# Reordering the last batch of a cross-attention kernel: sums ahead of value columns, small operations and a mask moved up

## The chip, the core and the metric

The kernel runs on one core of a Trainium2 chip. The metric is the device time of one launch in microseconds (us); three runs of the kernel before gave 453.07, 457.52 and 457.72, so its median is 457.52 us. All data are 32-bit floats. The engines have queues of their own[...]: TensorE (PE; loads of its stationary operand are shown apart as PEld), VectorE (DVE), ScalarE (ACT), GpSimd (POOL) and SyncE (SP), which here issues the DMA transfers.

## What is computed

For each of 8 batches: `S` = 112 queries with 320 channels attend to 371 text tokens and to 4 prompt tokens of a context of 375 tokens with 512 channels, in 20 heads of 16 channels.

```python
text_ehs, ip_ehs = encoder_hidden_states[:, :-4], encoder_hidden_states[:, -4:]
q, k_t, v_t = heads(hidden_states @ W_q), heads(text_ehs @ W_k), heads(text_ehs @ W_v)
probs_t = softmax(einsum('bhsd,bhtd->bhst', q, k_t) * attn_scale)
text_out = einsum('bhst,bhtd->bhsd', probs_t, v_t)
k_ip, v_ip = heads(ip_ehs @ W_k_ip), heads(ip_ehs @ W_v_ip)
attn_scores = einsum('bhsd,bhnd->bhsn', q, k_ip) * attn_scale
qsem = l2norm(einsum('bhst,bte->bhse', probs_t, text_ehs))
sem = einsum('bhse,bne->bhsn', qsem, l2norm(ip_ehs))
probs_ip = softmax(attn_scores + 0.5 * sem) * spatial_mask
ip_out = einsum('bhsn,bhnd->bhsd', probs_ip, v_ip)
out = (text_out + ip_out) @ W_out + b_out + hidden_states
```

The second softmax, over the four prompt tokens, needs the length of `qsem` for each query and head, and so a sum over all text tokens that is known only when a head's products are done.

## The kernel before

**Groups and products.** A batch's 20 heads are done in five groups (`g` = 0 to 4) of four heads each. `scores` (L573) multiplies queries by keys into one PSUM bank a head; `probabilities` (L591) takes the maximum (L595, VectorE), the exponent (L599, ScalarE) into the tile `p`, of which there are three buffers (L597), and sends it to the tile `xg` by a DMA a head (L602). When all four have landed, `transposed` (L606) makes one VectorE transpose of 128 by 1536 (L610). `multiplied` (L616) then does 12 blocks of four products (L629) on TensorE, each head into a bank of its own: columns 0 to 370 of a bank belong to the quadratic form behind the length of `qsem`, and the last 21, the "value columns", hold four prompt sums, the softmax's denominator `z` and the 16 text output channels. Its moving operand `u` holds the values of one group at a time; `placed` (L547) copies those of the next group over them on POOL, a third at a time, as soon as TensorE has done the blocks that read that third.

**After a group's products.** `value_sums` (L639) copies the value columns of each bank to `pvs` on ScalarE (L642). `reduced` (L673) multiplies columns 0 to 370 by `p` and sums them into `ss`, one custom VectorE instruction a head (L677). In the last batch some heads go another way, `shared` (L644): ScalarE copies value columns and bank out (L661, L662), POOL multiplies (L666), ScalarE sums (L670). VectorE and ScalarE never read one bank at the same time: whichever comes first in the program is waited for by the other.

**The end of a batch.** `finish` (L690) is a generator; each `next` or `run` issues one piece. Its pieces for a whole batch in the last batch's manner (`bd` given) are: (1) `xb`, the residual plus bias, on POOL, and `z2`, `rn` on VectorE; (2) a square root on ScalarE (L724), which needs a table load, and a load of the exponent's table after it; (3) six small VectorE operations from `zr` to `fu` (L741 to L748); (4) an exponent (L752); (5) three small VectorE operations up to the weights `w` (L756 to L760), and the division `divided` on POOL (L731); (6) a TensorE transpose of `w` and ScalarE's copy of it, `wT` (L768, L772); (7) products with the block diagonal `bd` into `ps_a` and ScalarE's copy `aT` (L778, L781, L789); (8) the output projection `ps_o` (L796); (9) `ob`, the sum with `xb`; (10) the transfer out. `ob` has one buffer. `own_channels` (L532) masks `bd`, the prompt values of batches 6 and 7, to block diagonals on POOL, by a memset and two selects.

**The last batch.** Batches 0 to 6 run in a loop with all engines in program order but POOL. For batch 7 POOL joins them (L1020), so every queue there holds the order of the program text, loop L1039 to L1090 and what follows it. That batch computes in group `g` the scores of group `g + 2` (`places`, L1045: after which block which heads), ends batch 6 in pieces (`run(before, ...)`) between its own, and does its own end in two parts: `first`, heads 0 to 15, begun after group 3, and `last`, heads 16 to 19, after group 4. `awake` (L366) is three multiplies whose result nobody uses.

Of the kernel before, what the change touches and what calls it, by code (L numbers as in the profile page):

```python
# [8 lines left out]
F32 = mybir.dt.float32  # L9
AF = mybir.ActivationFunctionType  # L10
ALU = mybir.AluOpType
# [9 lines left out]
def kernel(  # L21
# [503 lines left out]
        )  # L525

    def load_prompt_values_by_head():
        bd = io.tile([P, NT, E], F32, tag="ct", name="bd")[:HN, :2, :CP]
        nc.sync.dma_start(bd[:, :, :C], vipx.rearrange("b h n c -> (h n) b c"))
        return bd  # L530

# [74 lines left out]
    def transposed(b, g):  # L606

        xg = x_ring[(b * NG + g) % NX]
        xT = work.tile([P, BLK, P], F32, tag="xgT", name=f"xgT_{b}_{g}")
        nc.vector.transpose(  # L610
            xT.rearrange("p j (k q) -> p q j k", q=QN),
            xg.rearrange("p q (j k) -> p q j k", k=RG),
        )
        st[b]["xT", g] = xT
# [24 lines left out]
    def value_sums(b, g, a0=0):  # L639
        s = st[b]  # L640
        for h, ps in list(zip(groups[g], s["qd", g]))[a0:]:
            nc.scalar.copy(s["pvs"][:, h, :], ps[:S, TT:UW])  # L642

    def shared(b, g):  # L644

        s = st[b]
        some = list(enumerate(zip(groups[g], s["qd", g])))
        if b == B - 1:
            some = some[: GROUP - 1]
            t = work.tile([P, NE, TP], F32, tag="ctxT", name=f"shared_{b}_{g}")  # L650
            prods = [t[:S, a, :TT] for a, _ in some]
        else:

            some = some[: GROUP // 2]
            t = work.tile([S, NIP, H, D], F32, tag="wv", name=f"shared_{b}_{g}", bufs=1)
            t = t.rearrange("p n h d -> p (n h d)")
            prods = [t[:, a * TP : a * TP + TT] for a, _ in some]
        p = s["p", g]
        for a, (h, ps) in some:
            if b == B - 1:  # L660
                nc.scalar.copy(s["pvs"][:, h, :], ps[:S, TT:UW])  # L661
            nc.scalar.copy(prods[a], ps[:S, :TT])  # L662
        yield

        for a, _ in some:
            nc.gpsimd.tensor_tensor(prods[a], prods[a], p[:, a, :], ALU.mult)  # L666
        yield

        for a, (h, _) in some:
            nc.scalar.activation(prods[a], prods[a], AF.Copy, accum_out=s["ss"][:, h : h + 1])  # L670
        yield

    def reduced(b, g, a0=0):  # L673
        s = st[b]
        for a, (h, ps) in list(enumerate(zip(groups[g], s.pop(("qd", g)))))[a0:]:
            junk = small.tile([S, TT], F32, tag="junk", name=f"junk_{b}_{h}", bufs=1)
            nc.vector.tensor_tensor_reduce(  # L677
                out=junk,
                in0=ps[:S, :TT],
                in1=s["p", g][:, a, :],  # L680
                scale=1.0,
                scalar=0.0,
                op0=ALU.mult,
                op1=ALU.add,
                accum_out=s["ss"][:, h : h + 1],
            )
        del s["p", g]


    def finish(b, heads=(0, H), eng=None, late=False, bd=None):  # L690
# [16 lines left out]

        pvs = s["pvs"][:, part]
        if not late:
            if b == B - 1:  # L710

                s["xb"] = work.tile([P, NE, TP], F32, tag="ctxT", name=f"xb_{b}")[:S, 0, :C]
            else:
                s["xb"] = work.tile([S, C], F32, tag="xb", name=f"xb_{b}", bufs=1)
            nc.gpsimd.tensor_tensor(s["xb"], x_sb[:, b, :], bias_sb, ALU.add)
        z = pvs[:, :, NIP]

        z2 = sm("z2")
        nc.vector.scalar_tensor_tensor(z2, z, EPS * EPS, z, ALU.mult, ALU.mult)
        rn = sm("rn")  # L720
        nc.vector.tensor_tensor(rn, s["ss"][:, part], z2, ALU.max)
        yield

        nc.scalar.activation(rn, rn, AF.Sqrt)  # L724
        nc.scalar.preload_act_table(AF.Exp)
        zr = sm("zr")
        attn = attn_ring[b % 2]
        ah = attn[:, :C].rearrange("p (h d) -> p h d", d=D)[:, part]
# [1 line left out]
        def divided():  # L730
            eng.tensor_tensor(  # L731
                ah, pvs[:, :, NIP + 1 :], zr.unsqueeze(2).to_broadcast([S, n, D]), ALU.mult
            )

        if bd is None:
            nc.vector.reciprocal(zr, z)
            divided()
        yield

        if bd is not None:  # L740
            nc.vector.reciprocal(zr, z)  # L741
        nc.vector.reciprocal(rn, rn)
        fu = sm4("fu")
        nc.vector.tensor_tensor(fu, pvs[:, :, :NIP], over_ip(rn), ALU.mult)
# [13 lines left out]
        nc.vector.reciprocal(rx, sx)  # L758
        w = sm4("w")
        nc.vector.scalar_tensor_tensor(w, ex, sm_sb, over_ip(rx), ALU.mult, ALU.mult)  # L760
        if bd is not None:
            divided()
        yield

        i0, i1 = h0 * D // P, -(-h1 * D // P)
# [89 lines left out]
    def drain(*gens):  # L855
        for gen in gens:
            for _ in gen:
                pass
# [6 lines left out]
    def run(key, make, pieces=1):  # L865

        if key not in gens:
            gens[key] = make()
        for _ in range(pieces):
            next(gens[key], None)  # L870
# [98 lines left out]
    for n, (b, g) in enumerate(steps[:-NG]):  # L969
        coming = steps[n + LEAD]  # L970
        for j, _ in enumerate(multiplied(b, g)):
            for a in {0: (2, 3), 6: (0, 1)}.get(j, ()):
                scores(*coming, a)
                if j == 0:
                    probabilities(*coming, a)
            if j == 2:
                transposed(*steps[n + 1])
                if 1 <= g <= 3:
                    gram_to_groups(b + 1, {1: (0,), 2: (2,), 3: (3,)}[g])

                if g in (1, 2) and b > 0:
                    run(("f", b - 1), None)
        value_sums(b, g)
        if g == 2 and b > 0:
            run(("f", b - 1), None)
        for a in (0, 1):
            probabilities(*coming, a)
        if n == len(steps) - NG - 1:
            sums = shared(b, g)
            next(sums)  # L990
            reduced(b, g, 2)
        else:
            reduced(b, g)
        placed(*steps[n + 1])
        if g == 0 and b > 1:
            run(("f", b - 2), None)
        if g == 0:
            load_next(b + 2)
        elif g == 1:
            gram_to_groups(b + 1, (1,))  # L1000
        elif g == 3:
            values_to_groups(b + 1)
        if g == 1 and b == 0:
            run(("pp",), None)
        if (b, g) == (B - 3, 1):
            prompt_values_by_head()
        if (b, g) == (B - 2, 1):
            bd = load_prompt_values_by_head()
        if g == NG - 1 and b < B - 2:
            prompt_values(b)  # L1010
        between(b, g)
        if g == 1:
            values_to_dram(b + 1, nc.sync, 0, 2)
        if g == 2:
            values_to_dram(b + 1, nc.sync, 2)
# [23 lines left out]
    for g in range(NG):  # L1039
        if g == 1:  # L1040
            keys3 = last_keys(b, ps_qd.tile([P, 512], F32, tag="qd", name=f"ps_k_{b}_{FULL}"))
            next(keys3)
            coming(g, (3, 0))
            next(keys3)
        places = {0: {0: (2, 3), 1: (0, 1)}, 1: {0: (1, 2)}, 2: {1: (3, 0), 2: (1, 2)}}.get(g, {})  # L1045
        for j, _ in enumerate(multiplied(b, g)):
            coming(g, places.get(j, ()))
            if j != 2:
                continue
            drain(sums)  # L1050
            if g == 2:
                run(before, lambda: finish(b - 1, bd=bd[:, 0]))
            if g + 1 < NG:
                transposed(b, g + 1)
            if g == 3:
                run(before, None, 2)
                nc.scalar.preload_act_table(AF.Sqrt)
        if g <= LEAD:
            sums = shared(b, g)
            next(sums)  # L1060
            value_sums(b, g, GROUP - 1)
            reduced(b, g, GROUP - 1)
        else:
            value_sums(b, g)
            if g == NG - 1:
                run(before, None)
                next(first)
                run(before, None)
                nc.scalar.preload_act_table(AF.Sqrt)
                run(before, None)  # L1070
            reduced(b, g)
        if g + 1 < NG:
            placed(b, g + 1)
        if g <= LEAD:
            next(sums)
        if g == 0:
            drain(prompt_logits(b))
            run(("f", b - 2), None)
        if g == 1:
            prompt_values(b)  # L1080
        if g == 2:
            run(before, None)
        if g == 3:
            own_channels(bd)

            first = finish(b, (0, FULL * HC), bd=bd[:, 1])
            next(first)
            next(first)
            run(before, None)
            next(first)  # L1090
    last = finish(b, (FULL * HC, H), nc.vector, late=True)
    next(last)
    next(first)
    next(last)
    awake(3, end=True)
    next(first)
    for _ in range(2):
        next(last)
# [50 lines left out]
```

## Time and profile before

The profiled execution took 458.5 us, with a span of 456.8 us; TensorE's mean granted clock was 0.983 of full.

| engine | busy us | share of the span | instructions |
|---|---|---|---|
| PE | 440.0 | 96% | 5137 |
| PEld | 339.1 | 74% | 5137 |
| DVE | 309.2 | 68% | 651 |
| ACT | 193.1 | 42% | 540 |
| POOL | 109.6 | 24% | 262 |

The shares are means over stages. Batch 7's own products begin at 402.08 us and its five groups end at 407.5, 417.2, 422.9, 429.8 and 435.5; its transposes 1 to 4 start at 405.47, 414.31, 421.86 and 427.29. The chain that ended last gives PE 89%, ACT 4%, DVE 3% and DMA 2% of the span. Rows of a timeline hold the start, the length, engine, line and operation, what is written and read, how many were merged, and in brackets for how long the engine had been idle and what ended it. In a table of stretches the columns are said beside it.

### The profile page before, as it was taken

How to read it: one execution, taken by the hardware profiler on the slowest of the kernel's cores; microseconds unless marked ns; L12 is line 12 of the kernel's file. 1: busy time of each engine (PE TensorE's matmuls, PEld its weight loads, DVE VectorE, ACT ScalarE, POOL GpSimd, SP SyncE). 2: the span in 40 equal slices, each digit the busy share in tenths (PEclk: the TensorE clock that was granted, in tenths of full speed). 3: DMA queues.
4: the chain of work that ended last, by engine and by line, in shares of the span. 5: the costliest groups of instructions: out<-in, count | busy, mean ns of one | idle time of the engine just before them, and what ended most of it. 6: DMA issues, size and time to landing. Idle time of an engine off the chain costs nothing.

```text
span 456.8 us, 12979 instructions
## 1 busy us (share of the span) xinstructions
PE 440.0 (96%) x5137; PEld 339.1 (74%) x5137; DVE 309.2 (68%) x651; ACT 193.1 (42%) x540; POOL 109.6 (24%) x262
## 2 busy tenths in 40 slices
PE   8999999999999999999999999999999999999766
PEld 8757667887678877887778877888768777878743
DVE  3057356786676668786686668787677668876772
ACT  2263233345334353345335353435335353366651
POOL 4302200012061113322061112311150212344600
PEclk9999899999999999999999999999999999999967
DMA  8779764645646554545645554545655446643200
GB/s 240 190 173 257 172 162 110 142 135 157 166 124 156 148 136 140 140 138 158 169 118 148 150 155 140 138 128 156 170 140 130 134 122 167 154 116 111 63 0 25
DMA packets 52158, 64.83 MB, mean 142 GB/s; under 512 B 18370, under 2 KB 44146, under 8 KB 52098
## 3 DMA queue, kind: packets, MB, share of 16 engines
q1 hardware_dynamic: 51658, 63.45, 52.5%
q8 instruction: 40, 0.66, 0.6%
q10 hardware_dynamic: 440, 0.56, 0.4%
q14 instruction: 20, 0.16, 0.1%
HBM read 19.30 MB, written 5.32 MB: 54 GB/s over the span
## 4 chain that ended last, share of the span: by engine, by line
PE 89%; ACT 4%; DVE 3%; DMA 2%; POOL 1%; issue 1%; SPq 0%; DVEq 0%; POOLq 0%; ACTq 0%
PE ps_qd L629 40%; PE ps_v L480 14%; PE ps_k L447 9%; PE ps_g L411 8%; PE ps_s L582 4%; PE ps_q L303 3%; PE ps_c L353 2%; PE ps_o L849 2%; ACT p L599 1%; PE ps_g L383 1%; PE ps_vip L265 1%; PE ps_o L796 1%; PE ps_ip L562 1%; DMA vr<-vd 1%; DMA xg<-p 1%; DVE xgT L610 1%
## 5 line engine op out<-in xcount | busy, mean ns | idle before, releaser
L629 PE MATMUL ps_qd<-u,xgT 32*112 32x104 f32 (+11 forms) x3840 | 216.3, 351 | 4.0 <-ACT shared L662 2.0
L629 PEld LDWEIGHTS ps_qd<-u,xgT 32*112 32x112 f32 x3840 | 182.6, 172 | 39.3 <-issue 12.8
L595 DVE TENSOR_REDUCE nmx<-ps_s 112x1 f32<-112x371 f32 x160 | 77.6, 529 | 76.2 <-PE ps_s L582 76.2
L610 DVE STREAM_TRANSPOSE xgT<-xg 128x1536 f32<-128x1536 f32 x40 | 119.1, 2976 | 7.8 <-DMA xg<-p 6.8
L599 ACT ACTIVATE p<-ps_s,nmx 112x371 f32<-112x371 f32 x160 | 82.4, 572 | 63.3 <-DVE nmx L595 51.1
L677 DVE CUSTOM_DVE_ANT_0 junk<-ps_qd,p 112x371 f32<-112x371 f32 x149 | 80.8, 542 | 20.1 <-ACT pvs L642 4.4
L551 POOL COPY u<-vr 128x64 f32<-128x64 f32 x120 | 26.1, 239 | 176.3 <-PE ps_qd L629 119.6
L582 PE MATMUL ps_s<-kT,qm 32*112 32x371 f32 x320 | 63.5, 476 | 0.4 <-ACT p L599 0.4
L480 PE MATMUL ps_v<-wv_sb,ctxT 128*128 128x384 f32 (+1 forms) x192 | 63.5, 480 | 0.0
L480 PEld LDWEIGHTS ps_v<-wv_sb,ctxT 128*128 128x128 f32 x192 | 35.2, 190 | 19.7
L447 PE MATMUL ps_k<-ctxT,wk_sb 128*128 128x371 f32 x136 | 45.9, 482 | 0.0
L642 ACT COPY pvs<-ps_qd 112x21 f32<-112x21 f32 x151 | 16.0, 190 | 64.9 <-PE ps_qd L629 64.8
L411 PE MATMUL ps_g<-ctxT 128*128 128x375 f32 (+2 forms) x168 | 37.4, 379 | 0.0
L447 PEld LDWEIGHTS ps_k<-ctxT,wk_sb 128*128 128x128 f32 x136 | 25.1, 190 | 15.3 <-issue 0.5
L411 PEld LDWEIGHTS ps_g<-ctxT 128*128 128x128 f32 x168 | 28.1, 190 | 8.4
L582 PEld LDWEIGHTS ps_s<-kT,qm 32*112 32x112 f32 x320 | 25.6, 170 | 5.6 <-ACT kT L454 2.1
L312 DVE TENSOR_SCALAR qm<-ps_q,emask 128x224 f32<-128x224 f32 (+1 forms) x25 | 9.2, 400 | 24.3 <-PE ps_q L303 24.2
L487 ACT COPY vext<-ps_v 128x384 f32<-128x384 f32 (+1 forms) x24 | 11.2, 466 | 27.2 <-PE ps_v L480 26.7
L454 ACT COPY kT<-ps_k 128x371 f32<-128x371 f32 x17 | 8.0, 469 | 26.2 <-PE ps_k L447 26.2
L399 ACT ACTIVATE ug<-ps_g 128x375 f32<-128x375 f32 (+2 forms) x24 | 9.0, 377 | 23.0 <-PE ps_g L411 19.9
L818 POOL TENSOR_TENSOR wv<-vip,w 112x1280 f32<-112x1280 f32 x6 | 14.8, 2463 | 14.6 <-DVE w L760 14.6
L400 POOL TENSOR_TENSOR ug<-ug,half 128x128 f32<-128x128 f32 (+1 forms) x24 | 10.8, 452 | 29.8 <-ACT ug L399 29.8
(127 smaller groups left out, 342.3 us busy)
## 6 DMA issues: line engine op xcount, KB each, us to landing
xg<-p SPq DMA_DIRECT2D x160, 162.3 KB
u<-ug SPq DMA_DIRECT2D x128, 99.0 KB
ct<-in_ctx_dram SPq DMA_DIRECT2D x16, 256.0 KB
vip<-vipd SPq DMA_DIRECT2D x7, 560.0 KB
vr<-vd SPq DMA_DIRECT2D x32, 120.0 KB
vd<-vext SPq DMA_DIRECT2D x7, 320.0 KB
ct<-in_ctx_dram SPq DMA_DIRECT2D x8, 224.0 KB
vd<-vext SPq DMA_DIRECT2D x7, 160.0 KB
```

Of the source, the lines that this page charges most:

```text
L411: nc.tensor.matmul(ps[:, : T - t0], ctxT[:, e, t0 : t0 + P], ctxT[:, e, t0:T], start=(e == 0), stop=(e == NE - 1),)
L447: nc.tensor.matmul(ps[:, :TT], wk_sb[:, e, i * P : (i + 1) * P], s["ctxT"][:, e, :TT], start=(e == 0), stop=(e == NE - 1),)
L480: nc.tensor.matmul(ps[:, :w], ctxT[:, e, c * P : (c + 1) * P], wv_sb[:, e, :w], start=(e == 0), stop=(e == NE - 1),)
L551: nc.gpsimd.tensor_copy(region(b, c)[:, :, UV - c * P :], s["vr"][:, c * QN : (c + 1) * QN, g, :])
L582: nc.tensor.matmul(ps[:S, :TT], qm[a * RG : (a + 1) * RG, i, r, j * S : (j + 1) * S], s["kT"][a * RG : (a + 1) * RG, i, :], start=True, st ...
L595: nc.vector.tensor_reduce(nmx, ps[:S, :TT], AX.X, ALU.max, negate=True)
L599: nc.scalar.activation(p, ps[:S, :TT], AF.Exp, bias=nmx)
L610: nc.vector.transpose(xT.rearrange("p j (k q) -> p q j k", q=QN), xg.rearrange("p q (j k) -> p q j k", k=RG),)
L629: nc.tensor.matmul(banks[a][:S, j * RG : UW], xT[a * RG : (a + 1) * RG, j, :S], region(b, c)[a * RG : (a + 1) * RG, q, q * RG :], start=(j ...
L642: nc.scalar.copy(s["pvs"][:, h, :], ps[:S, TT:UW])
L677: nc.vector.tensor_tensor_reduce(out=junk, in0=ps[:S, :TT], in1=s["p", g][:, a, :], scale=1.0, scalar=0.0, op0=ALU.mult, op1=ALU.add, accu ...
L818: eng.tensor_tensor(wv, s["vip"][:, :, part], w.rearrange("p h n -> p n h").unsqueeze(3).to_broadcast([S, NIP, n, D]), ALU.mult,)
```

## The change

All of it concerns batch 7's loop and the pieces of batch 6 that run in it.

- `with_bias` is `xb`'s addition as a function of its own. Batch 7's `xb` goes to a free part of the tile that holds `bd`, not to a buffer with tag `ctxT`, and is made after group 0, with the mask of `bd`, which was made after group 3.
- Batch 6's end starts in group 1, was group 2; with `bd` given, `zr` and the division on POOL belong to its first piece, were in pieces 3 and 5. Square root and table loads come inside group 2, before ScalarE's copies of it; the small operations up to `fu` and the exponent after group 2's sums, ahead of transpose 4, were after it; `w` after transpose 4.
- In each group VectorE's sums are issued before ScalarE's value columns of the same banks.
- Group 2's scores of heads 3 and 0 move from after block 1 to after block 0, of heads 1 and 2 from block 2 to block 1.
- In group 3 one head is done by way of ScalarE and POOL, was none. ScalarE's sums of groups 1 and 2 come later.
- After the loop, the exponent of heads 0 to 15 stands before batch 6's `wT`, `awake` before the projection and not after it, and group 4's sums and value columns after all of this.

```diff
@@ load_prompt_values_by_head
-        bd = io.tile([P, NT, E], F32, tag="ct", name="bd")[:HN, :2, :CP]
+        t = io.tile([P, NT, E], F32, tag="ct", name="bd")
+        st[B - 1]["xb"] = t[:S, 2, :C]
+        bd = t[:HN, :2, :CP]
@@ shared
-    def shared(b, g):
+    def shared(b, g, n):
...
-        some = list(enumerate(zip(groups[g], s["qd", g])))
+        some = list(enumerate(zip(groups[g], s["qd", g])))[:n]
...
+    def with_bias(b):
+        nc.gpsimd.tensor_tensor(st[b]["xb"], x_sb[:, b, :], bias_sb, ALU.add)
@@ finish
+        if bd is not None:
+            nc.vector.reciprocal(zr, z)
+            divided()
+        yield
+
+        nc.scalar.activation(rn, rn, AF.Sqrt)
+        nc.scalar.preload_act_table(AF.Exp)
...
-        if bd is not None:
-            nc.vector.reciprocal(zr, z)
         nc.vector.reciprocal(rn, rn)
...
-        if bd is not None:
-            divided()
         yield
@@ the loop over the groups of the last batch
             next(keys3)
-        places = {0: {0: (2, 3), 1: (0, 1)}, 1: {0: (1, 2)}, 2: {1: (3, 0), 2: (1, 2)}}.get(g, {})
+            run(before, lambda: finish(b - 1, bd=bd[:, 0]))
+        places = {0: {0: (2, 3), 1: (0, 1)}, 1: {0: (1, 2)}, 2: {0: (3, 0), 1: (1, 2)}}.get(g, {})
         for j, _ in enumerate(multiplied(b, g)):
             coming(g, places.get(j, ()))
             if j != 2:
                 continue
-            drain(sums)
-            if g == 2:
-                run(before, lambda: finish(b - 1, bd=bd[:, 0]))
+            if g < LEAD:
+                drain(sums)
             if g + 1 < NG:
                 transposed(b, g + 1)
+            if g == 2:
+                run(before, None)
             if g == 3:
-                run(before, None, 2)
-                nc.scalar.preload_act_table(AF.Sqrt)
-        if g <= LEAD:
-            sums = shared(b, g)
+                run(before, None)
+        ahead = sums
+        if g < NG - 1:
+
+            n = GROUP - 1 if g <= LEAD else 1
+            sums = shared(b, g, n)
             next(sums)
-            value_sums(b, g, GROUP - 1)
-            reduced(b, g, GROUP - 1)
-        else:
-            value_sums(b, g)
-            if g == NG - 1:
-                run(before, None)
-                next(first)
-                run(before, None)
-                nc.scalar.preload_act_table(AF.Sqrt)
-                run(before, None)
-            reduced(b, g)
-        if g + 1 < NG:
+            reduced(b, g, n)
+            if g <= LEAD:
+                value_sums(b, g, n)
             placed(b, g + 1)
-        if g <= LEAD:
             next(sums)
         if g == 0:
+            own_channels(bd)
+            with_bias(b)
             drain(prompt_logits(b))
             run(("f", b - 2), None)
         if g == 1:
             prompt_values(b)
         if g == 2:
-            run(before, None)
+            run(before, None, 2)
+            drain(ahead)
+            nc.scalar.preload_act_table(AF.Sqrt)
         if g == 3:
-            own_channels(bd)
+            drain(ahead)
+            drain(sums)
+            value_sums(b, g, n)
 
             first = finish(b, (0, FULL * HC), bd=bd[:, 1])
-            next(first)
-            next(first)
-            run(before, None)
-            next(first)
+            for _ in range(3):
+                next(first)
+    next(first)
+    run(before, None)
+    nc.scalar.preload_act_table(AF.Sqrt)
+    run(before, None)
+    awake(3, end=True)
+    run(before, None)
+    reduced(b, g)
+    value_sums(b, g)
     last = finish(b, (FULL * HC, H), nc.vector, late=True)
     next(last)
     next(first)
     next(last)
-    awake(3, end=True)
     next(first)
```

## The prediction

> **What bounds the kernel now.** The page gives TensorE 96% of the span and 89% of the chain that ended last, so over most of the span only TensorE's work counts. I therefore cut the end of the span into stretches between TensorE's bursts (us from the start, then busy time and count of PE, PEld, DVE, ACT, POOL, then the granted clock, DMA share and GB/s):
>
> ```profile
> 417.50:424.97 7.47, 5.43 (x105) 4.75 (x105) 5.69 (x9) 5.62 (x22) 4.89 (x9) 1.00 0.47 145
> 424.97:430.42 5.45, 4.80 (x97) 4.16 (x97) 3.68 (x5) 4.78 (x11) 3.11 (x8) 1.00 0.16 47
> 430.42:435.46 5.04, 5.04 (x96) 4.92 (x96) 3.08 (x6) 1.96 (x6) 3.46 (x4) 1.00 0.01 3
> 435.46:440.29 4.83, 0.87 (x4) 0.63 (x4) 4.11 (x18) 2.05 (x7) 0.71 (x1) 0.78 0.00 0
> 440.29:446.83 6.54, 6.01 (x17) 4.44 (x18) 4.50 (x22) 3.47 (x5) 0.00 (x0) 0.50 0.00 0
> 446.83:453.88 7.05, 5.39 (x23) 3.35 (x21) 2.71 (x8) 0.96 (x4) 0.00 (x0) 0.89 0.07 20
> ```
>
> The last group of products ends at 435.46; 21.3 us follow in which no engine is full, and in nearly half of them the clock is at 0.50. Next the chain of waits and the timeline of each engine there:
>
> ```profile
> 421.12 3.57 SPq L602 DMA_DIRECT2D xg<-p  x4
> 423.89 3.28 DMA xg<-p
> 427.29 2.98 DVE L610 STREAM_TRANSPOSE xgT<-xg 128x1536 f32<-128x1536 f32 x1 [1.34 <-DMA xg<-p]
> 430.51 0.87 DVE L744 TENSOR_TENSOR fu<-pvs,rn 112x80 f32<-112x80 f32 x1
> 431.42 1.04 DVE L745 SCALAR_TENSOR_TENSOR fu<-fu,ipl 112x80 f32<-112x80 f32 x1
> 433.38 0.27 ACT L752 ACTIVATE ex<-fu 112x80 f32<-112x80 f32 x1 [3.57 <-DVE fu L748]
> 433.67 1.28 ACT L1057 ACT_TABLE_LOAD   x1
> 434.96 0.41 ACT L642 COPY pvs<-ps_qd 112x21 f32<-112x21 f32 x4
> 435.17 0.55 DVE L677 CUSTOM_DVE_ANT_0 junk<-ps_qd,p 112x371 f32<-112x371 f32 x1 [1.82 <-ACT pvs L642]
> 439.14 0.38 PE L768 MATMUL ps_wT<-ident,w 112*80 112x112 f32 x1 [3.69 <-DVE w L760]
> 443.29 3.54 PE L796 MATMUL ps_o<-wo_sb,aT 128*112 128x320 f32 x6 [0.53 <-ACT aT L789]
> 448.54 0.21 ACT L752 ACTIVATE ex<-fu 112x16 f32<-112x16 f32 x1
> 453.39 0.49 DVE L809 TENSOR_TENSOR ob<-ps_o,xb 112x320 f32<-112x320 f32 x1 [2.13 <-DMA out_dram<-ob]
> ```
>
> The reader is to see one knot. Group 3's bank is full at 429.77, yet its first sum starts at 435.17: VectorE stands behind ScalarE's value columns (L642), these behind a table load and batch 6's exponent, and that behind batch 6's five small operations, which VectorE makes only after transpose 4 (427.29). So batch 7's sums, batch 6's weights `w`, and TensorE's next work are all late; TensorE sits 3.69 us, and then works at half clock.
>
> [...]
>
> **The change, part by part.** Only batch 7's loop changes (and small operations of batch 6 in it); up to 407.5 nothing differs. No transfer moves: SP's queue keeps its order, and the tail keeps its six table loads.
>
> 1. *POOL.* The mask of `bd` (0.20 + 2.08) and `xb` of batch 7 (0.88) leave 430 to 433 and stand after group 0's products (end 410.86), then `xb` and the division of batch 6 (0.89 + 0.75): 4.8 us, less overlaps of some 0.1, to 415.5. POOL was idle there from 410.86 to 415.18. The first value copy of group 2 comes 0.3 late; its second waits for TensorE until 416.64 anyway. Cost 0; without that cover at most 0.3.
> 2. *Start of batch 6's end* (z, rn, zr, some 0.6): VectorE is idle 411.4 to 413.4. Cost 0. It takes 0.4 from before transpose 3 (421.86).
> 3. *Sums ahead of value columns.* In group 0 the columns now wait for the sum, to 409.3; ScalarE is next wanted at 411.11, so 0. Sum 3 of group 1 can run at 417.3, not 418.70, and scores move up one block. But that block's first score needs the bank that ScalarE copies until 418.59, where before it started at 418.77. So 0.1 to 0.2; with step 2 transpose 3 ends some 0.5 earlier, and group 3's products too.
> 4. *None of that reaches group 4.* Its exponents start at 420.53 because `p` has three buffers and POOL's product of group 1 frees one at 420.43; SP then issues four transfers at some 0.8 each and the last lands at 427.17. All unchanged. So transpose 4 ends at 430.27 and TensorE's last group at 435.46 as before. Gain of steps 1 to 4: 0.
> 5. *ScalarE's new order from 422.4:* load, rn, load (2.83, by 425.38 to 428.21) to 425.2; seven copies of group 2 (1.53) to 426.7; ex (0.27) to 427.0; three sums of group 1 (1.5) to 428.5; load (1.28) to 429.8; two copies of group 3 (0.55) to 430.3; four sums (2.1) to 432.4. These need POOL's products, to 428.5 for group 2, and one more (0.9) from 430.3 to 431.2: in time. Group 3's first bank goes this way, so VectorE has one sum (0.70) less.
> 6. *Five small operations ahead of transpose 4.* rn is there at 423.9; VectorE has made transpose 3 and one sum by 424.9. Nine cases of each line exist, most with POOL elsewhere:
>
> ```profile
> L744 DVE TENSOR_TENSOR fu<-pvs,rn x9: 175/242/871, 122.5 to 445.0; 112x80 f32<-112x80 f32 x7, 112x64 f32<-112x64 f32 x1, 112x16 f32<-112x16 f32 x1
> L745 DVE SCALAR_TENSOR_TENSOR fu<-fu,ipl x9: 176/242/1037, 122.8 to 445.2; 112x80 f32<-112x80 f32 x7, 112x64 f32<-112x64 f32 x1, 112x16 f32<-112x16 f32 x1
> ```
>
>    The 871 and 1037 are those that ran beside POOL's mask. Uncovered: 5 x 0.25 + gaps, to 426.4; all slow: 3.2, to 428.1. The transfer lands at 427.17. I take 0; the bounds are 0 and +0.9.
> 7. *Group 3's sums.* After transpose 4: batch 6's w (0.96) to 431.2, three sums (0.70 each) to 433.3, last value columns 0.2; z starts at 433.5, before at 437.73: **-4.2**. ScalarE's 432.4 is inside. Exponent of 16 heads: z + 0.43, a 1.28 load beside VectorE's chain of zr, rn, fu, mx, fu (1.8): 435.8, before 440.71.
> 8. *TensorE* no longer waits for w (431.2): wT right after 435.46, ScalarE's copy after ex at 436.0 (before 439.96). Idle gaps stay under 1.5 us, so the clock should stay full: ps_a from 436.3, 2.5 us at half, so 1.25, to 437.5 (before 442.78). The three filler multiplies now stand beside ScalarE's copy (0.64); ps_o takes 1.80 (the full-clock row of batch 5, L849 x6) and not 3.54, to 440.0.
> 9. *Group 4.* Four sums (2.7) from 435.8 to 438.45, columns to 438.65; before they ended at 443.16. z to the last small fu takes 2.7 (443.08 to 445.80): 441.4, **-4.4**.
> 10. *Last exponent.* Before it waited from 445.80 to 448.54, since ScalarE stood at wT (L772) behind ps_o at half clock and the fillers. Now wT is copied at 440.8 (behind a load): exponent at 441.45, another **-2.7**.
> 11. From the last exponent to the end: 456.8 - 448.54 = 8.3, a chain of VectorE and two output transfers through one buffer `ob`. Unchanged: 449.7.
>
> Sum: 4.4 + 2.7 = **7.1 us**. Against the profiled execution's own 458.5 that is 451.4. That execution lies 1.0 above the median 457.52, so **450.5** in the terms of the median.
>
> **Rivals.** [...] *(B) Transpose 4 becomes late by the small operations* (0.9, step 6), or ScalarE's longer queue holds group 3's columns by another 1: gain 5.2 to 6.2, 451.3 to 452.3. *(C) It doesn't do what it says:* another wait of the tail, such as the load before the last wT or bank order, takes most of the gain: 455 to 457. Against it: each queue above has its slack listed. *(D) Slower:* the 4.8 us block put into POOL's queue ahead of group 2's value copies. Spans on POOL are rough, and there it runs beside VectorE. It is covered while it ends by some 417.0, since three copies of 0.24 then still precede group 1's products at 417.77; beyond, each microsecond delays the products, the exponents that wait for their buffer at 420.43, and so transpose 4. It decides against the change when the slip passes 7.1, a block of 6.1 + 7.1 = 13.2 us; at 16 us the time is 460.3. Speaking against: the same instructions but one `xb` took 3.8 us beside a busy VectorE, 430.16 to 433.94.
>
> **How the numbers follow.** Main case 0.70 (450.5, own range 448 to 452.5); A 0.13; B 0.08; C 0.06; D 0.03. The three runs before spread from 453.07 to 457.72, and a median of the changed kernel may catch the lower kind: 446. Range 446 to 455. Within 1% means 452.9 to 462.1, about what a measurement of this kernel can't tell from no change. Faster by more: 0.76 (main, B, half of A, less the spread); within 1%: 0.22 (C, half of A, the spread, most of D); slower: 0.02.
>
> **What would show it.** TensorE's last product still ends near 435.5; L677 no longer waits on value columns; batch 6's five small operations lie between transposes 3 and 4, ending before 427.3; no 3.7 us hole of TensorE after its last product; clock at 1.00 to the end; ps_o near 1.8; exponent and end 7 earlier. I am wrong if transpose 4 starts after 428, if POOL's first value copy of group 2 comes after 416.7, or if the clock falls.

## The result, and the profile after

| | before | changed |
|---|---|---|
| median of 12 runs, us | 457.73 | 451.24 |
| lowest to highest, us | 453.07 to 458.27 | 450.07 to 455.31 |
| profiled execution: its time and span, us | 458.5, 456.8 | 450.23, 448.5 |
| mean granted clock of TensorE in it | 0.983 | 0.998 |
| end of the last product to end of span, us | 21.34 | 14.03 |

The medians lie 6.5 us apart. The ratio of the times is 0.9884, with a 95% interval of 0.9852 to 0.9916: the changed kernel is faster by 1.2%, some 5.3 us. This is less than the medians say, since the ratio is one of means: two quick runs of the kernel before (453.07 and 453.26) and a slow one of the changed kernel (455.31) count in it and hardly in the medians. The two profiled executions lie 8.3 us apart in span. Of that, 0.87 us was there before the change begins: batch 7's products start at 401.21 us and not at 402.08, since the mean clock from about 34 to 102 us was 1.00 in one record and 0.98 in the other, where both kernels do the same. So I compare from the last product on, where nothing of that comes in: 7.31 us less.

The stretches between TensorE's bursts in the changed kernel (the columns as in the prediction's table of stretches):

```profile
423.58:429.43 5.85, 4.80 (x97) 4.17 (x97) 4.50 (x10) 5.81 (x19) 3.29 (x6) 1.00 0.21 60
429.43:434.47 5.04, 5.04 (x97) 4.99 (x98) 3.78 (x15) 3.74 (x14) 1.60 (x2) 1.00 0.02 5
434.47:438.00 3.53, 3.07 (x22) 2.67 (x23) 2.79 (x13) 2.71 (x9) 0.00 (x0) 1.00 0.00 0
438.00:442.00 4.00, 3.25 (x16) 2.02 (x15) 3.12 (x16) 2.30 (x5) 0.00 (x0) 1.00 0.00 0
```

The clock (third number from the end) stays at 1.00 where it was 0.78 and 0.50, and TensorE is busy in 87% of the 3.53 us after its last product (three filler multiplies, from 436.58 on, among it), where it was busy in 18% of 4.83. The timeline of the same kernel, VectorE, ScalarE and TensorE together:

```profile
424.04 0.24 DVE L745 TENSOR_TENSOR fu<-pvs,rn 112x80 f32<-112x80 f32 x1
425.79 0.33 ACT L753 ACTIVATE ex<-fu 112x80 f32<-112x80 f32 x1
426.27 3.00 DVE L612 STREAM_TRANSPOSE xgT<-xg 128x1536 f32<-128x1536 f32 x1 [1.17 <-DMA xg<-p]
430.10 0.51 DVE L761 SCALAR_TENSOR_TENSOR w<-ex,sm_sb,rx 112x80 f32<-112x80 f32 x1 [0.47 <-DVE rx L759]
430.53 0.53 DVE L677 CUSTOM_DVE_ANT_0 junk<-ps_qd,p 112x371 f32<-112x371 f32 x1
434.39 0.29 PE L767 MATMUL ps_wT<-ident,w 112*80 112x112 f32 x1
434.93 0.26 ACT L753 ACTIVATE ex<-fu 112x64 f32<-112x64 f32 x1 [0.27 <-DVE fu L749]
437.27 1.87 PE L795 MATMUL ps_o<-wo_sb,aT 128*112 128x320 f32 x6
440.23 0.21 ACT L753 ACTIVATE ex<-fu 112x16 f32<-112x16 f32 x1 [0.38 <-DVE fu L749]
445.09 0.49 DVE L808 TENSOR_TENSOR ob<-ps_o,bd 112x320 f32<-112x320 f32 x1 [2.13 <-DMA out_dram<-ob]
```

Line numbers have moved by one or two, and `bd` in the last row is the tile that now holds batch 7's `xb` too. The reader is to see the knot undone. Batch 6's `fu` and `ex` lie ahead of transpose 4, which still waits for its DMA. `w` and group 3's first sum follow the transpose, at 430.10 and 430.53 and without a wait for ScalarE; they came at 438.70 and 435.17. `wT` follows the last product at once, where TensorE had stood for 3.69 us. The projection takes 1.87 us, was 3.54. The last exponent comes at 440.23, 0.10 us after the last `fu` has ended (2.74 before). What is left is the last row: the second sum into `ob` still waits 2.13 us until the first one's transfer out has freed the buffer.

### The profile page after: what moved, and what is told of

Its sections match the earlier page's. It is cut to its first block, busy times and chain, and to the rows that moved or that the text cites. A ratio compares the mean times of both kernels' runs of the same rounds, so it can differ in the third digit from the quotient of the medians.

```text
span 448.5 us, 12974 instructions
## 1 busy us (share of the span) xinstructions
PE 435.1 (97%) x5137; PEld 336.2 (75%) x5137; DVE 308.2 (69%) x649; ACT 194.1 (43%) x543; POOL 110.0 (25%) x263
## 4 chain that ended last, share of the span: by engine, by line
PE 88%; DVE 3%; ACT 3%; DMA 3%; issue 1%; POOL 1%; SPq 1%; DVEq 0%; ACTq 0%
PE ps_qd L631 41%; PE ps_v L480 14%; PE ps_k L447 9%; PE ps_g L411 8%; PE ps_s L584 4%; PE ps_q L303 3%; PE ps_c L353 2%; PE ps_o L848 2%; DMA xg<-p 1%; ACT p L601 1%; PE ps_g L383 1%; DVE junk L677 1%; PE ps_ip L564 1%; DVE xgT L612 1%; PE ps_k L463 1%
```

## The experiments

Each run is compared with runs of the kernel before on the same chip; "tail" is the time from the end of the last product to the end of the span, in the profiled execution. On these chips the medians of the kernel before go from 456.95 to 457.36 us, and the result above has 457.73; so where medians from different chips are set side by side, differences under 0.8 us say nothing.

### How much is the clock alone: TensorE kept busy, order as before

The kernel before, with `awake` for fifteen filler multiplies after its last product; nothing else is moved.

```diff
             if g == NG - 1:
+                awake(15, end=True)
                 run(before, None)
```

> The kernel before with 15 idle multiplies on TensorE behind its last group of products, to keep its clock up through the 3.7 us hole. Theory (the order of ScalarE and VectorE makes the tail, the clock is a part of it): clock 1.00 to the end, ps_o near 1.8 us instead of 3.54; the last exponent then stands at VectorE's last small operation (445.8 before) instead of at wT (448.5), so 2.7 us shorter and no more. Rival (the clock is nearly the whole gain): 5.5 to 7 us shorter, like the changed kernel.

Median 455.05 us, ratio 0.9949 (0.9935 to 0.9963). The tail is 18.43 us, 2.91 shorter. Stretches of this kernel:

```profile
435.00:440.29 5.29, 4.66 (x37) 4.26 (x38) 4.54 (x20) 2.11 (x8) 0.71 (x1) 1.00 0.00 0
440.29:446.83 6.54, 5.52 (x30) 3.98 (x30) 5.19 (x25) 4.20 (x8) 0.00 (x0) 1.00 0.01 3
```

The clock holds, the projection takes 1.87 us, and the last exponent comes at 445.12, at once after its `fu`. It holds in the other runs too, as far as their mean clock tells: 0.996 to 1.000 in all 16, against 0.986 to 0.993 in the 43 of the kernel before. So of the 7.31 us of the tail 2.9 are the clock's (2.0 in the medians); the other 4.4, by subtraction, need the order of VectorE and ScalarE. They coincide with the two terms of the prediction's sum, 2.7 and 4.4.

### One part alone: only the small operations moved up

The kernel before, in which batch 6's five small operations, the exponent and the table load behind it stand after group 2, and no other part is changed: value columns still come ahead of sums, and the mask stays after group 3.

```diff
-            if g == 3:
-                run(before, None, 2)
-                nc.scalar.preload_act_table(AF.Sqrt)
...
         if g == 2:
-            run(before, None)
+            run(before, None, 3)
+            nc.scalar.preload_act_table(AF.Sqrt)
```

> The kernel before with one part of the change alone: batch 6's five small operations and its exponent issued ahead of transpose 4. Theory: VectorE's first sum of group 3 starts about 4 us earlier although transpose 4 comes about 1 us later (the square root stands behind ScalarE's copies here); no hole of TensorE over 3 us, so full clock; 5.8 us shorter in all. Rival (the sums behind the value columns are the knot, not the small operations): under 2 us shorter.

Median 451.58 us in 4 runs (451.43 to 451.72), 5.5 us shorter (5.8 expected); ratio 0.9884 (0.9855 to 0.9914): that of the whole change. The tail is 13.89 us. VectorE's timeline of this kernel:

```profile
427.49 0.24 DVE L748 TENSOR_TENSOR fu<-fu,mx 112x80 f32<-112x80 f32 x1
427.67 2.95 DVE L610 STREAM_TRANSPOSE xgT<-xg 128x1536 f32<-128x1536 f32 x1
431.03 0.54 DVE L677 CUSTOM_DVE_ANT_0 junk<-ps_qd,p 112x371 f32<-112x371 f32 x1 [0.41 <-ACT pvs L642]
```

Here transpose 4 no longer waits for the DMA but for `fu`, and so starts 1.4 us later than in the changed kernel; its last product ends at 435.81, not 434.47. Of either, 0.3 us was there when batch 7's products began (401.52 and 401.21). This part brings the whole gain of the tail. For the rest of the change it leaves at most the 0.9 us by which the time from the start of batch 7's products to the end differs (48.2 and 47.3 us). In the medians 0.3 us of that is left, too little to tell from nothing.

### The same part taken back out of the change

The changed kernel, with those operations behind transpose 4 again.

```diff
             if g == 3:
+                run(before, None, 2)
+                nc.scalar.preload_act_table(AF.Sqrt)
                 run(before, None)
...
         if g == 2:
-            run(before, None, 2)
             drain(ahead)
-            nc.scalar.preload_act_table(AF.Sqrt)
```

> The changed kernel with that one part undone: the five small operations, the exponent and the square root's table behind transpose 4 again. Theory: group 3's last value columns about 2.2 us later and so the end, 2.2 us longer if the clock holds (TensorE's hole becomes about 3.0 us), 4.4 longer if it falls. Rival (clock alone): nothing if the clock holds.

Median 454.86 us in 20 runs (452.23 to 456.38), ratio 0.9946 (0.9927 to 0.9964); the tail is 18.58 us, 4.55 longer. From TensorE's timeline of this kernel, and then a stretch of it:

```profile
439.04 0.77 PE L780 MATMUL ps_a<-wT,bd 80*128 80x112 f32 x2 [2.40 <-ACT wT L771]
```

```profile
440.00:443.00 3.00, 3.00 (x15) 2.92 (x14) 1.50 (x8) 1.29 (x8) 0.00 (x0) 0.50 0.00 0
```

ScalarE copies `wT` only behind an exponent, which waits for sums whose value columns stand behind batch 6's exponent at 431.94. TensorE has a hole of 2.40 us and half clock behind it: this execution took the branch in which the clock falls. In the medians the order costs 3.6 us, over half of the gain. The runs differ: two of the 20 had a mean clock of 0.999, and their times, 452.23 and 452.72 us, lie 1.4 and 1.9 us above 450.87, the median of the changed kernel's five runs at 0.998 or 0.999. The two at 0.986 took 456.19 and 456.38 us, and the others, at 0.990 to 0.996, lie between. So 1.4 to 1.9 us of the cost are there at full clock (2.2 expected), and most of the rest goes with the clock.

The two runs also say that the parts overlap and do not add. Alone, the move brings the whole gain; but where it is missing, the rest of the change still takes the tail from 21.34 to 18.58 us.

### Value columns ahead of sums, with ScalarE's new order kept

The changed kernel, with `value_sums` issued ahead of `reduced` in every group.

```diff
-            reduced(b, g, n)
             if g <= LEAD:
                 value_sums(b, g, n)
+            else:
+                drain(ahead)
+                value_sums(b, g, n)
+            reduced(b, g, n)
...
         if g == 3:
-            drain(ahead)
             drain(sums)
-            value_sums(b, g, n)
...
-    reduced(b, g)
     value_sums(b, g)
+    reduced(b, g)
```

> The changed kernel with value columns ahead of VectorE's sums of the same banks again in all groups, the rest as changed. Theory: group 3's sums start about 0.5 later and group 4's sums wait for ScalarE, which is at aT until 437.2, so they start near 437.5 instead of 434.8: 3.1 us longer. Rival (the order within a bank costs nothing, as ScalarE would be early enough): within 0.5 us of the changed kernel.

Median 456.94 us in 12 runs, ratio 1.0012 (0.9985 to 1.0038): 5.7 us above the changed kernel, by the ratio its whole gain. The timeline of this kernel:

```profile
425.51 0.23 ACT L644 COPY pvs<-ps_qd 112x21 f32<-112x21 f32 x1
425.77 0.54 DVE L677 CUSTOM_DVE_ANT_0 junk<-ps_qd,p 112x371 f32<-112x371 f32 x1 [2.55 <-ACT pvs L644]
428.13 2.91 DVE L612 STREAM_TRANSPOSE xgT<-xg 128x1536 f32<-128x1536 f32 x1
431.20 6.73 PE L631 MATMUL ps_qd<-u,xgT 32*112 32x392 f32 x96 [3.02 <-DVE sx L757]
440.50 0.55 DVE L677 CUSTOM_DVE_ANT_0 junk<-ps_qd,p 112x371 f32<-112x371 f32 x1 [2.95 <-ACT pvs L644]
```

The last row is what I had expected: group 4's sums wait for ScalarE, and start 2.6 us after the last product where they started 0.3 us after it, and the last exponent is 2.0 us later behind the last product. What I had missed is in the rows above it.

The change put two table loads, of 1.28 us each, ahead of ScalarE's copies of group 2. If group 2's sum must wait for the copy of its value columns, it waits for the loads too; VectorE stands 2.55 us, and the small operations and transpose 4 are queued behind it. Counted from the start of batch 7's products, transpose 4 starts 2.1 us later than in the changed kernel; TensorE has a hole of 3.02 us, and the clock falls in the last group of products (0.75 on average), which take 6.73 us and not 5.04. By the end of that group 3.7 us are lost. A third part, 1.2 us, is lost behind the last exponent, where the clock is at 0.51 on average from 446 to 452 us.

So sums ahead of columns is the condition on which ScalarE's new order is safe. In the run with the small operations alone the table loads stay behind those copies, and columns first costs VectorE waits of 0.54 and 0.41 us. What sums first would bring in the kernel before, with nothing else changed, no run here shows.

### Three placements undone

The changed kernel, with group 2's scores after blocks 1 and 2, `wT` of batch 6 ahead of the exponent of heads 0 to 15, and `awake` behind the projection, each as before.

```diff
-        places = {0: {0: (2, 3), 1: (0, 1)}, 1: {0: (1, 2)}, 2: {0: (3, 0), 1: (1, 2)}}.get(g, {})
+        places = {0: {0: (2, 3), 1: (0, 1)}, 1: {0: (1, 2)}, 2: {1: (3, 0), 2: (1, 2)}}.get(g, {})
...
-    next(first)
     run(before, None)
+    next(first)
     nc.scalar.preload_act_table(AF.Sqrt)
-    run(before, None)
+    run(before, None, 2)
     awake(3, end=True)
-    run(before, None)
```

> The changed kernel with three of its edits undone that the prediction costed at next to nothing: group 2's scores one block later, wT ahead of the exponent of heads 0 to 15, the fillers behind the projection. Theory: within 0.3 us of the changed kernel, clock at 1.00 to the end. Rival (one of them holds the clock, or the fillers in front of the last wT hold the last exponent as they did in the kernel before): 1.5 to 2.5 us longer.

Median 450.62 us in 4 runs, ratio 0.9859 (0.984 to 0.9878); tail 14.04 us against 14.03. Together they are worth nothing that shows.

### The mask left late

The changed kernel, with the mask of `bd` and batch 7's `xb` after group 3 again.

```diff
         if g == 0:
-            own_channels(bd)
-            with_bias(b)
...
             value_sums(b, g, n)
+            own_channels(bd)
+            with_bias(b)
```

> The changed kernel with the mask of the prompt values and batch 7's xb behind group 3 again. Theory: POOL then works beside VectorE's small operations from 430.5 to 433.7, which cost it some 0.5 us (0 to 1.0), nothing else changes. Rival (the mask beside the small operations was a large part of the tail, as the 0.87 and 1.04 us rows of before look): 2 us longer or more.

Median 450.88 us in 4 runs, ratio 0.9877 (0.9848 to 0.9905); the tail is 14.5 us, 0.5 longer, and TensorE waits 1.06 us for `wT` where it waited 0.46. That is the size expected, in the profiled execution; the medians can't show it.

### What covers POOL's block

The changed kernel, with `xb` of batch 7 made seven times in a row, 5.7 us more in POOL's queue ahead of group 2's value copies.

```diff
             own_channels(bd)
-            with_bias(b)
+            for _ in range(7):
+                with_bias(b)
```

> The changed kernel with batch 7's xb made seven times instead of once (the same values), 5.0 us more in POOL's queue ahead of group 2's value copies; this is rival D of the prediction with its block at 9.6 us. Theory: the cover ends some 2 us behind the block as it is, so the products of group 1 and with them transpose 4 come 3.3 to 3.5 us later, and the end too; 5.4 if TensorE's hole ahead of group 2 lets the clock fall. Rival (POOL has slack): under 1 us longer.

Median 455.71 us in 12 runs, ratio 0.9971 (0.9949 to 0.9993): 4.5 us above the changed kernel, and 6.3 in span (454.8 and 448.5). From the timeline of POOL and TensorE of this kernel, and a stretch:

```profile
419.75 0.74 POOL L727 TENSOR_TENSOR attn<-pvs,zr 112x320 f32<-112x320 f32 x1
420.72 1.66 PE L631 MATMUL ps_qd<-u,xgT 32*112 32x392 f32 x8 [4.08 <-POOL u L553]
```

```profile
420.72:426.00 5.28, 5.28 (x36) 3.74 (x40) 1.95 (x5) 1.40 (x3) 2.95 (x5) 0.50 0.00 0
```

The block ends at 420.49, the copies of values come behind it, and TensorE waits 4.08 us for the first. This is the prediction's rival D, and its place is right: in the changed kernel the block ends at 414.53, the copies follow from 414.47 to 416.75, and no product waits for them. D put the limit at 417.0, in the times of the kernel before, whose batch 7 starts 0.60 us later than here (402.08 and 401.48). So the block ends 4.1 us beyond it, and at D's price, 1 us for each, that is 4.1 us. The medians say 4.5, and the two ratios, 0.9971 and 0.9884, some 4.0: the price is about right.

In the profiled execution the loss is larger, 6.0 us from the start of batch 7's products to the end (53.3 and 47.3 us). Behind the hole TensorE ran at half clock for the 5.28 us of the stretch, which by an estimate, half of it, is worth 2.6 us; and transpose 4 waited for the small operations, two of which ran beside POOL and took 0.90 and 0.63 us. The mean clock is 0.990 to 0.994 in all 12 runs, so it probably fell in all. Why the medians lose less than this execution stays open.

### The changed kernel again, and what is left after it

The last four share their runs of the kernel before. The first is the changed kernel unaltered; each of the others adds to the one ahead of it. The first addition puts batch 6's `ob` into the time in which VectorE waits for the last exponent, so that its transfer has left the one buffer sooner:

```diff
     for _ in range(2):
         next(last)
+    drain(gens[before])
     for _ in range(2):
         next(first)
     for _ in range(4):
         next(last)
-    drain(gens[before])
```

The second moves the reciprocal and the division of heads 16 to 19 behind that exponent:

```diff
-        if bd is None:
+        if bd is None and not late:
...
         nc.scalar.activation(ex, fu, AF.Exp)
+        if late:
+            nc.vector.reciprocal(zr, z)
+            divided()
```

The third has the last transfer of group 4's exponents issued by ScalarE and not by SP:

```diff
-        nc.sync.dma_start(
+        eng = nc.scalar if (b, g, a) == (B - 1, NG - 1, 2) else nc.sync
+        eng.dma_start(
```

> The changed kernel unaltered, on the chip of the next three, to compare them with. Theory and rival alike: ratio to the kernel before 0.985 to 0.990.

> The changed kernel with batch 6's output sum and its transfer issued while VectorE waits for the last exponent, and not behind the last prompt sums. Theory (the end is held by the one buffer of ob: the last sum waits 2.1 us for the first transfer): the last sum starts after TensorE's last product, some 0.65 us earlier; span 0.65 shorter. Rival (TensorE's last projection is as late as the buffer): nothing.

> As the run with the early output sum, and the reciprocal and division of heads 16 to 19 moved from ahead of their small operations into the wait for the last exponent. Theory (VectorE alone sets the time between the last product and the last exponent): another 0.35 us shorter, 1.0 under the changed kernel in the span. Rival (ScalarE's table load and wT set the last exponent): no further gain.

> As the run before, and the last of group 4's four transfers issued from ScalarE instead of SP, whose issues follow each other at 0.9 us. Theory (the landing of that transfer starts transpose 4): transpose 4 starts up to 0.9 us earlier, and 0.3 to 0.6 arrives at the end. Rival (ScalarE's own queue, delayed by the issue, takes it back, or the transfer lands no earlier): no gain or up to 0.8 longer.

| | median us (runs) | ratio to before | tail us |
|---|---|---|---|
| changed kernel again | 451.30 (5) | 0.9868 (0.9836 to 0.99) | 14.1 |
| `ob` early | 450.06 (4) | 0.9839 (0.9807 to 0.9872) | 13.0 |
| and the division in the wait | 449.62 (6) | 0.9836 (0.9802 to 0.9869) | 14.4 |
| and one issue on ScalarE | 449.46 (4) | 0.9826 (0.9792 to 0.9859) | 13.4 |

With `ob` early, VectorE's timeline has

```profile
445.21 0.49 DVE L808 TENSOR_TENSOR ob<-ps_o,bd 112x320 f32<-112x320 f32 x1 [1.72 <-PE ps_o L848]
```

so the last sum waits for TensorE's last projection and no longer for the buffer: the end of the chain has changed hands, and 1.1 us of the tail are gone (0.65 expected). The span of this execution is not shorter (448.6 us, the changed kernel's 448.3), since transpose 4 waited longer for its transfer and started 25.9 us after batch 7's first product, not 25.0; the median is 1.2 us lower.

With the second addition the last exponent comes 5.23 us after the last product, not 5.56: the 0.35 expected. Its tail is longer all the same in the profiled execution, because there the clock fell: from 430 to 448 us it is 0.91 on average, in the changed kernel 0.96, and TensorE's last projections took 2.12 and 1.32 us, where the same counts took 1.33 and 0.79.

```profile
441.79 2.12 PE L798 MATMUL ps_o<-wo_sb,aT 128*112 128x320 f32 x4 [0.43 <-ACT aT L791]
```

With the third, ScalarE spends 0.93 us on the issue and its table load waits for that; transpose 4 wins 0.4 us, counted from batch 7's first product, and the tail is 0.4 us longer than with `ob` early. The last version has the lowest median of all, 1.8 us (0.4%) under the changed kernel, and its slowest run, 450.00 us, is not slower than the quickest of the changed kernel's five, 450.04; but the intervals of all four ratios overlap, so that it is better is likely and not shown.

## Why the prediction was right

The forecast was 450.5 us, the median is 451.24. By its own steps, with times from the start of transpose 4 (427.29 before, 426.27 after) or from the last product's end, so that the earlier start doesn't count:

| term | predicted | measured |
|---|---|---|
| `z` of heads 0 to 15 earlier (step 7) | 4.2 | 4.0 |
| last product to first `ps_a` with `wT` (8) | 0.84 | 0.91 |
| `ps_o`, batch 6 (8) | 1.80 | 1.87 |
| last small `fu` earlier (9) | 4.4 | 4.65 |
| wait of the last exponent gone (10) | 2.7 | 2.64 |
| last exponent to the end (11) | 8.3, unchanged | 8.27 |
| sum of steps 9 and 10 | 7.1 | 7.29 |

**The chain it named is the one.** Undoing the small operations' move, alone, loses over half of the gain (3.6 of 6.5 us in the medians, 4.55 of 7.31 in the tail), and making it, alone, brings all of it. Group 3's sums, the weights and the last exponent moved as said, and the clock stayed at 1.00 in the profiled execution up to TensorE's last product. Step 5 held as well: ScalarE's four sums ended at 431.43, which is 432.3 in the times of the kernel before (432.4 predicted). Step 8 goes from gaps under 1.5 us to a full clock, and step 10 builds on it; that is an estimate of mine, and no run shows it. What the runs showed: behind the last product the gaps were 0.46 us at most in the changed kernel, at a clock of 1.00, and 0.43 us at most with the division in the wait, where the clock fell in the tail.

**Steps 1 to 4 and 6, costs of nothing, held,** one of them by little. Step 1: POOL's block took 4.6 us (4.8 predicted), and its cover is the one named, as lengthening it showed. Step 2 was mis-sized: "z, rn, zr, some 0.6" took 1.8, from 410.52 to 412.35, because step 1 had just put the mask beside them: with the mask left late the same three took 0.8, from 410.14 to 410.95. The maximum that follows still waited 0.18 us for TensorE, so the cover sufficed with 0.18 left, not with more than 1; that the slip cost nothing was luck. Step 3: a score waited 0.26 us for ScalarE's copy of its bank (0.1 to 0.2 predicted), hidden. Step 6: the five small operations took 0.24 each and ended at 425.10, 1.17 us ahead of the transfer; taking the uncovered end of its bounds was right. The late end was reached where the small operations are moved alone: there they hold transpose 4.

**Where it saw too little.** Step 3 priced sums ahead of columns by what it adds, 0.1 to 0.2. It did not ask what ScalarE's new order (step 5) would cost without it; that is 5.7 us. A list of parts, each with its price, hid that two of them belong together. And rivals D and A (half clock in the tail all the same, a gain of 4.9 us) were taken as separate cases, though a slip of POOL makes a hole, 4.08 us above, and the trace shows half clock behind it, 0.50 for 5.28 us: D's 1 us for each microsecond of slip was 1.1 by the medians above, but 1.5 in the profiled execution.

**Two slips of the reading.** The sum, 457.52 less 7.1, is 450.4 and not 450.5. And that no engine is full in the tail does not hold for 440.29 to 446.83, where TensorE, at half clock, is busy for 6.01 of 6.54 us; there its own work is the limit, which is why the clock counts.

**The runs' spread.** The profiles lie 7.3 us apart in the tail, the ratio says 5.3 (3.8 to 6.8). The runs of the kernel before differ in mean clock, from 0.983 (its profiled execution) to 0.993, so the tail need not be 21.3 us in all of them. The changed kernel's slower runs have a lower mean clock: 455.31 us at 0.987, 452.98 at 0.993, against 450.07 to 450.95 in five runs at 0.998 or 0.999. Where these lost it is not known, since only one execution of each kernel left a trace. The traces of other runs show two places: between 40 and 100 us (a mean clock of 0.97 in the kernel before, in the small operations late and in the three placements undone, of 1.00 in the others) and in the tail (the division in the wait, 1.4 us). Either can make the 0.7 us between forecast and median.

## What to carry to other kernels

Before work is moved ahead on one engine, ask who on the other engines waits for what it is moved past: two table loads ahead of a copy were free only because the reader of the same bank no longer stood behind that copy. At the end of a kernel, price a hole of TensorE twice, as the wait and as the clock behind it (here 3.69 us and 0.50), and try filler multiplies in the old order to see how much of a gain is only the clock. Undo and do each part alone: here one move of a few lines equals, in its ratio, the whole change, and yet without it the rest still keeps part of the gain.

## What the runs showed of the hardware

**Holes and the clock.** Here a clock of 0.50 to 0.53 followed holes of TensorE of 3.69 us (the kernel before), 3.02 (value columns first), 4.08 (POOL's block), and also of 2.40 (small operations late) and 2.15 (value columns first, 442.31 to 444.46). It did not follow holes of 2.04 (the kernel before, ahead of 424.97), 1.83 (`ob` early) and 1.40 (POOL's block, ahead of 435.26).

The clock also fell without such a hole. In the run with the division in the wait it did so in the tail (0.91 on average from 430 to 448 us, in the changed kernel 0.96), though TensorE had not waited longer than 1.22 us since 427. In the kernel before it was at 0.51 on average from 49.0 to 52.5 us, in a row of products without a hole since 36, among them 24 of only 32 columns (from 46.07 on, 2.77 us); in the changed kernel it stayed at 1.00 at both places, with the same products. Why is not shown. So "no hole over 3 us, so full clock", as expected of the small operations alone, came true there and is no rule: behind holes of 2.40 and 2.15 us the clock fell, and from 49.0 to 52.5 us it fell in one execution and held in another.

**VectorE beside POOL.** A small operation of 112 by 80 took 0.24 us alone and 0.87 to 1.04 beside POOL's mask; with the mask moved, `z` and `rn` took 0.58 and 0.95, and with the mask late again 0.34 and 0.18. Two pairs of maxima out of PSUM, one beside the start of the mask and one beside the additions of `xb`, kept their 0.99 us. The mask's cost went with it to its new place; only the cover differs.
